# Attention values of a Macaron block: three full products per unit become four full products and two pairs over 64 rows

## The chip, the core and the metric

The kernel runs on one core of one Trainium2 chip. The metric is the device time of one execution in microseconds (us); the median of three runs is given. Inside a core the engines are TensorE (PE; its weight loads are listed apart as PEld), VectorE (DVE), ScalarE (ACT), GpSimd (POOL) and SyncE (SP), whose queue issues the DMAs. Durations of single instructions come from one profiled execution.

## The reference

Four sequences of 256 tokens, 512 features, all float32, go through half a feed-forward layer, an attention layer and half a feed-forward layer, each behind a layer norm without weights:

```python
x = x + 0.5 * ffn(layernorm(x), ...)     # base matrix + 8 low-rank experts, the top 2 chosen per token
x = x + attn(layernorm(x), wq, wk, wv, wo)
x = x + 0.5 * ffn(layernorm(x), ...)
```

The attention is what matters here. It has 32 query heads of 128 features and 8 key heads, so that 4 query heads share the keys and values of one key head. Queries and keys are rotated (rope). Token `i` sees token `j` only if `j <= i` and `j > i - 128`:

```python
scores = einsum("bqhgd,bshd->bhgqs", qg, k) * 128 ** -0.5
allowed = (j <= i) & (j > i - 128)
attn = softmax(where(allowed, scores, -inf))
out = einsum("bhgqs,bshd->bqhgd", attn, v).reshape(B, S, 4096) @ wo
```

## The kernel before, in words

The tokens are worked on in two halves `h` of two sequences each. In each half the attention goes over the 8 key heads `g`; a `group` is one `(h, g)` with its 4 query heads, and a `unit` is one `(h, g, b)`: one group and one sequence `b` of the half. There are 32 units. Products with large weights (queries, keys, values of the projection, output projection, feed-forward) are made by Strassen's scheme in Winograd's form: seven products of half size, with the sums made on POOL and DVE.

For one unit, `scores` makes the products of queries and keys in 8 blocks of 32 queries by 4 heads (128 rows). The first 4 blocks (queries 0 to 127) see the keys from 0 up to their own block; the other 4 (queries 128 to 255) see a window of 128 keys that ends in their own. `picked` and `copy_predicated` shift the windows so that a key keeps its place in its row: in a block of the second half, a column holds either the weight of an old key (0 to 127) or that of the new key 128 higher, never both. `exponentials` (ACT) writes them to `probs`, `normalize` (POOL) scales, and `turn_blocks` turns squares of 32 by 32 (DVE) and stores them to a scratch tensor `kept` in DRAM. `fetch` loads them back to `turned`, which has 128 keys on partitions, then 4 heads, 8 blocks and 32 queries; four DMAs on SP's queue, one for each 32 partitions.

`values` then multiplies by the values. `vS` holds for each sequence the values `v0` of tokens 0 to 127 and, after `difference`, the differences `v1 - v0`. Queries 0 to 127 need one product of 512 columns, `turned` blocks 0 to 3 with `v0`, in the bank `oa`. Queries 128 to 255 take two, in the bank `ob`: all of blocks 4 to 7 with `v0`, and `part` with `v1 - v0`. `part` is what `split` keeps of blocks 4 to 7: the entries that belong to new keys. `split` runs on POOL for `b == 0` (L807) and on DVE for `b == 1` (L812). Two ACT copies (L832) bring the banks to `oT`, from which `outputs` makes the sums (POOL, L126) and the seven products of the output projection (L852).

The order on PE and DVE within the units is written out by hand: in a unit with `b == 0` the letters of `order` interleave queries of the next group, the waiting output products (`late`) and the next scores; in a unit with `b == 1` the keys or the values of the projection for the next groups come in between. POOL and ACT follow the order of the code as well. Around `values` a unit runs

```python
        if not parts:
            part()
        ...
        oT = values(h, g, b, *parts)
        if b == 0 and n + 1 < len(groups):
            first, *begun = keys(*groups[n + 1]) if n % 2 == 1 else project_values(*groups[n])
            first()
```

`turn` (transposes, store and `fetch`) comes some 9 us of PE work ahead of `values` in a unit with `b == 1`. Between the two halves of the tokens `sum_tokens` makes the token sums of the second half: `t1` and `t3` on POOL, `t2` and `t4` on DVE.

Of the kernel before, what the change touches and what calls it, by code (L numbers as in the profile page):

```python
# [12 lines left out]
F32 = mybir.dt.float32  # L13
AF = mybir.ActivationFunctionType
ALU = mybir.AluOpType
AX = mybir.AxisListType

P = 128
# [20 lines left out]
def macaron_kernel(  # L39
# [154 lines left out]

    def by_heads(dst, make):
        make(dst, 0)
        other = sb.tile(list(dst.shape), F32, tag="by_heads", bufs=1, name=f"{dst.name}_hi")
        for j in range(1, G):
            make(other, j * BLK)
            nc.gpsimd.tensor_copy(dst[ts(j, BLK), :], other[ts(j, BLK), :])  # L200
# [35 lines left out]
    for c in range(1, NB):  # L236
        nc.gpsimd.memset(turned[ts(c, BLK), :, :c, :], 0.0)


    old = const.tile([P, NB, BLK], F32, name="old")  # L240
    nc.gpsimd.memset(old, 1.0)
    nc.gpsimd.affine_select(
        out=old, in_=old, compare_op=ALU.is_gt,
        fill=0.0, base=0, pattern=[[-BLK, NB], [-1, BLK]], channel_multiplier=1,
    )
    new = const.tile([P, NB, BLK], F32, name="new")
    nc.gpsimd.tensor_scalar(new, old, -1.0, 1.0, ALU.mult, ALU.add)

    rank = const.tile([P, E], F32, name="rank")
    for e in range(E):  # L250
# [18 lines left out]
    def scale(t, tag):  # L269
        if (tag, t) not in moments:  # L270
            measure(t, tag)
        mv, std = moments[tag, t]
        std = std or deviation(t, tag, mv)
        rstd = sb.tile([P, 1], F32, tag="rstd", bufs=4, name=f"rs_{tag}_{t}")
        nc.vector.reciprocal(rstd, std)
        xc = sb.tile([P, D], F32, tag="xc", bufs=3, name=f"xc_{tag}_{t}")
        if tag == "f1":
            shift = sb.tile([P, 1], F32, tag="shift", bufs=4, name=f"sh_{tag}_{t}")
            nc.vector.scalar_tensor_tensor(shift, mv[:, 0:1], -1.0, rstd, ALU.mult, ALU.mult)
            cols = slice(D // 2 if t < 2 else 0, D)  # L280
            if t < 2:
                lo = slice(0, D // 2)
                nc.vector.tensor_scalar(xc[:, lo], xt[t][:, lo], mv[:, 0:1], rstd, ALU.subtract, ALU.mult)
            nc.scalar.activation(xc[:, cols], xt[t][:, cols], AF.Identity, bias=shift, scale=rstd)
        else:
            nc.vector.tensor_scalar(xc, xt[t], mv[:, 0:1], rstd, ALU.subtract, ALU.mult)
        if far(t, tag):
            nc.vector.transpose(xc, xc)
            away = dram.tile([KC, P, P], F32, tag="away", name=f"away_{tag}_{t}")
            nc.sync.dma_start(  # L290
                out=away.rearrange("c p x -> p c x"), in_=xc.rearrange("p (c x) -> p c x", c=KC)
            )
            xc = away
        moments[tag, t] = xc

    def far(t, tag):
        return tag == ("a" if t >= TPH else "f2")
# [56 lines left out]
    def ffn(tiles, tag, then):  # L354
# [22 lines left out]
        def narrow(i):  # L377
            t = tiles[i]
            if i == 0:
                state["hl"] = sb.tile([P, TPH, E * R + E], F32, tag="hl", name=f"hl_{tag}_{t0}")[:, :n, :]  # L380
            pa = score_bank(f"pa_{tag}_{t}")
            for c in range(KC):
                nc.tensor.matmul(  # L383
                    pa[:, : E * R + E], x_of(i, c), ar_sb[:, c, :],
                    start=(c == 0), stop=(c == KC - 1),
                )
            nc.scalar.copy(state["hl"][:, i, :], pa[:, : E * R + E])
# [84 lines left out]
        def gated():  # L472
            hl = state["hl"]
            pt = ps.tile([P, n, P], F32, tag="s", bufs=4, name=f"ph_{tag}_{t0}")
            for i in range(n):
                nc.tensor.transpose(pt[:, i, :], hl[:, i, : E * R], ident)
            state["ht"] = sb.tile([P, TPH, P], F32, tag="ht", bufs=1, name=f"ht_{tag}_{t0}")
            nc.scalar.copy(state["ht"][:, :n, :], pt)

        def leave(i):  # L480
            bank, t = po.pop(i), tiles[i]
# [71 lines left out]
    def add(dst, bank, other):  # L553
        nc.vector.tensor_tensor(dst, bank, other, ALU.add)
# [111 lines left out]
    def project_values(h, g):  # L666
# [36 lines left out]
        def others():  # L703
            product(2, c11)
            product(4, c21)
            add(v21, c21, u2)
            product(3, c12)
            nc.scalar.copy(v11, c11)
            add(v12, c12, u2)
            difference(h, g)  # L710

        return first, both, second, others

# [71 lines left out]
    def turn_blocks(pr, name, c):  # L785

        if c == 0:
            kept[name] = dram.tile([P, NB, 2 * NB * BLK], F32, tag="kept", name=f"kept_{name}")
        if True:
            w = pr[:, c : c + 2].rearrange("p c n k -> p (c n k)")  # L790
            nc.vector.transpose(w, w)  # L791
            nc.sync.dma_start(
                out=kept[name][:, c : c + 2, :], in_=pr[:, c : c + 2].rearrange("p c n k -> p c (n k)")
            )

    def fetch(name):
        heads = kept.pop(name).rearrange("(j k) c x -> k j c x", j=G)
        for c in range(NB):
            nc.sync.dma_start(
                out=turned[ts(c, BLK), :, c:, :].rearrange("p j n q -> p j (n q)"),  # L800
                in_=heads[:, :, c, c * BLK :],
            )

    def split(h, g, b):
        part = sb.tile([P, G, NB, BLK], F32, tag="part", bufs=1, name=f"part_{h}_{g}_{b}")
        if b == 0 or (h, g) == groups[-1]:
            nc.gpsimd.affine_select(  # L807
                out=part, in_=turned[:, :, NB:, :], compare_op=ALU.is_ge, fill=0.0, base=0,
                pattern=[[0, G], [BLK, NB], [1, BLK]], channel_multiplier=-1,
            )  # L810
        else:
            nc.vector.tensor_tensor(  # L812
                part, turned[:, :, NB:, :], new.unsqueeze(1).to_broadcast([P, G, NB, BLK]), ALU.mult
            )
        return [turned[:, :, :NB, :]], [turned[:, :, NB:, :], part]

    def difference(h, g, tiles=slice(None)):

        pairs = vS[h, g].rearrange("p (b i) f -> p b i f", i=2)[:, tiles]
        nc.vector.tensor_tensor(pairs[:, :, 1], pairs[:, :, 1], pairs[:, :, 0], ALU.subtract)  # L820

    def values(h, g, b, p0, p1):
        oT = sb.tile([HD, G, S], F32, tag="oT", bufs=4, name=f"oT_{h}_{g}_{b}")
        v = vS[h, g - g % 2]
        cols = ts(g % 2, HD)
        for i, parts in enumerate((p0, p1)):
            po = (score_bank, mm_bank)[i](f"o{'ab'[i]}_{h}_{g}_{b}")
            for n, part in enumerate(parts):
                nc.tensor.matmul(  # L829
                    po, v[:, 2 * b + n, cols], part, start=(n == 0), stop=(n == len(parts) - 1)  # L830
                )
            nc.scalar.copy(oT[:, :, ts(i, P)], po.rearrange("p (j q) -> p j q", j=G))  # L832
        return oT

    def outputs(h, g, b, oT):
# [162 lines left out]
    def run(queue, n):  # L998
        for _ in range(min(n, len(queue))):
            queue.popleft()()  # L1000
# [24 lines left out]
    for u, (h, g, b) in enumerate(units):  # L1025
# [11 lines left out]
        def turn_half(c):  # L1037
            once(f"t{c}{ahead[-1]}", lambda: turn_blocks(ahead[0], ahead[-1], c))
# [9 lines left out]
        fill(left, 0)  # L1048
        if left == 1:
            nc.scalar.activation(root, eps, AF.Sqrt)  # L1050
        parts = []

        def look_ahead(at=u + 1):
            nonlocal ahead
# [4 lines left out]
            add_sums(h - 1, BPH - 1, nc.gpsimd, slice(-2, None))  # L1059
            sum_weights("v", *groups[n])  # L1060

        def part(at=(h, g, b)):
            parts.extend(split(*at))

        if b == 0 and n < len(groups):

            order = {0: "1n6kTvD2U75tS4r3n", 4: "1Eyn6TaW2U7cyXx5dtSy4re3yVn"}[len(late)]
            steps = queries(*groups[n], nc.scalar.copy, ends)  # L1070
            steps |= {
                "y": lambda: run(late, 1), "r": invert, "n": level, "S": look_ahead,
                "E": lambda: exponentials(*ahead, which=range(NB, 2 * NB)),
                "D": lambda: difference(0, 0, slice(1)),
                "W": lambda: sum_o_weights(h, g, ("t3", "t1")), "X": lambda: sum_o_weights(h, g, ("t2",)),
                "x": between_halves if (h, g) == groups[NKV + 1] else None,
                "V": lambda: sum_o_weights(h, g, ("t4",)), "v": lambda: project_v(0, 0, 2),
                "k": lambda: sum_weights("k", *groups[2]), "a": lambda: fill(left, 1),
                "T": lambda: turn_half(0), "U": turn, "t": part, "c": None, "d": None, "e": None,
            }  # L1080

            if g == NKV - 2 and h + 1 < NHALF:
                more_tokens = sum_tokens(h + 1, *(nc.gpsimd, nc.vector) * 2)
                steps |= {"c": more_tokens[3], "d": more_tokens[1], "e": more_tokens[2]}
            for step in order:
                if steps[step]:
# [2 lines left out]
        elif b == 1 and n + 1 < len(groups):  # L1089
# [24 lines left out]
            elif n % 2 == 0 and n + 2 < len(groups):  # L1114
                load_v(*groups[n + 2])
            run(late, len(late) - 1)
            for t in shifted:
                norm_attn(t, scaled=True)
        else:
# [15 lines left out]
            load_q(*groups[n + 1])  # L1135
        if b == 0 and 1 < n < len(groups):
            load_o(*groups[n])
        if not parts:
            part()
        fill(left, 2)  # L1140
        run(late, len(late) - 1)
        early = ahead[-1] == "{}_{}_{}".format(*units[u + 1]) if left > 1 else False
# [7 lines left out]
        if u == 0:  # L1150
            project_v(0, 0, 3)
            load_v(*groups[2])
        oT = values(h, g, b, *parts)
        if u == 0:
            difference(0, 0, slice(1, 2))
        if b == 0 and n + 1 < len(groups):

# [79 lines left out]
```

## Time and profile before

| | |
|---|---|
| median of 3 runs | 740.63 us (740.61 to 741.09) |
| profiled execution | 740.92 us, of which the span from first to last instruction is 739.2 us |
| granted TensorE clock | 1.0 |
| DVE, POOL, ACT busy | 76%, 76%, 26% of the span |
| 16 DMA engines, busy share of the main queue | 35.4% |

The span is what the views divide; 1.7 us lie around it. A product in float32 appears in the trace as two records of MATMUL, each behind a weight load of its own: the product of 512 columns in `oa` occurs 32 times and has 64 records. Records overlap at their ends, so the duration of a record is longer than the distance from one start to the next; the distance is what a product costs in a busy stretch.

### The profile page before, as it was taken

Reading aid. Unit: us, or ns where it says so; the run is one execution under the profiler, and the core shown is the slowest. Engines: PE = TensorE matmul, PEld = TensorE weight load, DVE = VectorE, ACT = ScalarE, POOL = GpSimd, SP = SyncE. Lnnn points to the kernel's source line nnn. Section 1 sums busy time; section 2 is a strip of 40 time slices with the busy share of each in tenths; the row PEclk is TensorE's granted clock in tenths of the full one; section 3 lists DMA queues with packets and bytes.
Section 4 is the critical chain, followed back from the end, with each engine's and each line's share of the span. In section 5 each row is a group of like instructions: output and inputs, shape, how many; then the busy total and the mean of one; then the engine's idle time right before and its main releaser. Section 6 shows DMA issues by size and latency. Waiting matters only on the chain.

```text
span 739.2 us, 11048 instructions
## 1 busy us (share of the span) xinstructions
PE 728.7 (99%) x3606; PEld 603.3 (82%) x3606; DVE 562.5 (76%) x1297; ACT 195.1 (26%) x724; POOL 562.1 (76%) x613
## 2 busy tenths in 40 slices
PE   8999999999999999998999999999999999999998
PEld 6878888888888888886888888888888888888766
DVE  5797895878786878778677867586877867795877
ACT  5520223332222212130222233222123031222331
POOL 6878878777968686859878699868686878976753
PEclk9999999999999999999999999999999999999999
DMA  9301251424245433625142424242332415433201
GB/s 315 141 1 37 89 177 44 155 65 152 92 155 137 149 98 107 186 69 187 53 167 70 137 83 152 81 166 80 118 129 68 150 53 177 116 124 84 71 29 58
DMA packets 78249, 83.58 MB, mean 113 GB/s; under 512 B 21232, under 2 KB 50928, under 8 KB 78192
## 3 DMA queue, kind: packets, MB, share of 16 engines
q1 hardware_dynamic: 78192, 82.87, 35.4%
q8 instruction: 29, 0.48, 0.3%
q14 instruction: 28, 0.23, 0.1%
HBM read 61.88 MB, written 20.97 MB: 112 GB/s over the span
## 4 chain that ended last, share of the span: by engine, by line
PE 84%; POOL 6%; DVE 5%; issue 3%; DMA 1%; SPq 0%; ACT 0%; DVEq 0%; POOLq 0%
PE q L575 24%; PE y L852 22%; PE ob L829 7%; PE v L684 6%; PE k L632 6%; PE sb L753 4%; PE sa L739 3%; PE oa L829 3%; PE p_f L419 3%; PE po_f L419 2%; PE po_f L482 1%; PE y L894 1%; POOL x L393 1%; PE pa_f L383 1%; PE pv L720 1%
## 5 line engine op out<-in xcount | busy, mean ns | idle before, releaser
L531 POOL TENSOR_TENSOR qT<-ra_q,rb_q 128x512 f32<-128x512 f32 x64 | 81.8, 1279 | 74.8 <-DVE rb_q L525 74.8
L525 DVE TENSOR_TENSOR rb_q<-q,sin_sb 64x512 f32<-64x512 f32 x128 | 88.1, 688 | 1.7
L772 ACT ACTIVATE probs<-probs,mx 128x32 f32<-128x32 f32 (+3 forms) x128 | 44.7, 351 | 144.8 <-DVE mx L742 144.8
L779 POOL TENSOR_TENSOR probs<-probs,sm 128x512 f32<-128x512 f32 x64 | 65.7, 1046 | 6.1 <-DVE sm L1031 6.1
L869 DVE TENSOR_TENSOR x<-y,x 128x256 f32<-128x256 f32 (+1 forms) x62 | 34.2, 551 | 41.5 <-PE y L852 41.3
L852 PE MATMUL y<-wot,oT 128*128 128x256 f32 x248 | 63.7, 379 | 0.4 <-DVE rb_q L525 0.4
L852 PE MATMUL y<-wo,oT 128*128 128x256 f32 x248 | 63.7, 379 | 0.0
L832 ACT COPY oT<-oa 128x512 f32<-128x512 f32 x32 | 18.7, 585 | 169.1 <-PE oa L829 169.1
L852 PE MATMUL y<-wo,oTs 128*128 128x256 f32 x244 | 62.6, 379 | 0.0
L575 PE MATMUL q<-xs,wq 128*128 128x256 f32 x256 | 60.6, 379 | 0.2 <-DVE rb_k L525 0.2
L575 PE MATMUL q<-xs,wqs 128*128 128x256 f32 x256 | 60.6, 380 | 0.0
L575 PE MATMUL q<-xa,wq 128*128 128x256 f32 x256 | 60.5, 379 | 0.0
L575 PEld LDWEIGHTS q<-xa,wq 128*128 128x128 f32 x256 | 48.5, 190 | 12.5 <-issue 4.1
L575 PEld LDWEIGHTS q<-xs,wqs 128*128 128x128 f32 x256 | 48.5, 190 | 7.3 <-PE y L852 0.4
L575 PEld LDWEIGHTS q<-xs,wq 128*128 128x128 f32 x256 | 48.5, 190 | 7.0 <-issue 0.5
L791 DVE STREAM_TRANSPOSE probs<-probs 128x512 f32<-128x512 f32 x64 | 43.7, 700 | 10.8 <-POOL probs L779 10.4
L852 PEld LDWEIGHTS y<-wo,oTs 128*128 128x128 f32 x244 | 46.4, 190 | 6.3
L852 PEld LDWEIGHTS y<-wot,oT 128*128 128x128 f32 x248 | 45.8, 190 | 6.5 <-POOL wot L171 0.8
L852 PEld LDWEIGHTS y<-wo,oT 128*128 128x128 f32 x248 | 45.9, 190 | 5.3
L523 DVE TENSOR_TENSOR ra_q<-q,cos_sb 128x512 f32<-128x512 f32 x64 | 43.9, 686 | 6.3 <-PE q L575 2.0
L772 ACT ACTIVATE probs<-sb,mx 128x128 f32<-128x128 f32 x128 | 44.6, 357 | 0.0
L126 POOL TENSOR_TENSOR oTs<-oT 128x256 f32<-128x256 f32 x31 | 22.9, 740 | 23.5 <-ACT oT L832 23.5
(220 smaller groups left out, 1726.7 us busy)
## 6 DMA issues: line engine op xcount, KB each, us to landing
wq<-in_wq_dram SPq DMA_DIRECT2D x16, 1024.0 KB, 5.6
wo<-in_wo_dram SPq DMA_DIRECT2D x16, 1024.0 KB, 5.2
kept<-probs SPq DMA_DIRECT2D x64, 256.0 KB, 2.2
wk<-in_wk_dram SPq DMA_DIRECT2D x8, 512.0 KB, 4.3
wv<-in_wv_dram SPq DMA_DIRECT2D x8, 512.0 KB, 4.1
turned<-kept SPq DMA_DIRECT2D x32, 128.0 KB, 2.6
turned<-kept SPq DMA_DIRECT2D x32, 112.0 KB, 2.9
turned<-kept SPq DMA_DIRECT2D x32, 96.0 KB, 2.6
```

The costliest lines, as they stand in the source:

```text
L419: nc.tensor.matmul(bank[:, ts(i, D // 2)], lhs[j][m - 1][:, c, :], weights["bs"][m - 1][:, c, :], start=(m in (1, 5, 2, 4) and c == 0), st ...
L523: nc.vector.tensor_tensor(twice(a), twice(src), angle(cos_sb), ALU.mult)
L525: nc.vector.tensor_tensor(twice(b[o : o + half, :]), twice(src[i : i + half, :]), angle(sin_sb[o : o + half, :]), ALU.mult,)
L531: nc.gpsimd.tensor_tensor(dst, view(a), view(b), ALU.add)
L575: nc.tensor.matmul(bank[:, ts(j, S)], w[:, c, ts(j, HD)], x[:, c], start=(new and j == 0 and c == 0), stop=(c == 1), skip_group_check=True,)
L632: nc.tensor.matmul(dst, w[n - 1][:, c, :], x[n - 1][:, c], start=(start and c == 0), stop=(c == 1), skip_group_check=True,)
L684: nc.tensor.matmul(bank[:, i, :], x[n - 1][:, c, i, :], w[n - 1][:, c, :], start=(start and i == 0 and c == 0), stop=(c == 1), skip_group_ ...
L772: nc.scalar.activation(dst, src, AF.Exp, bias=mx[:, n : n + 1], scale=scale, accum_out=sm[:, n : n + 1])
L779: nc.gpsimd.tensor_tensor(w, w, sm.unsqueeze(1).unsqueeze(3).to_broadcast([P, 2, 2 * NB, BLK]), ALU.mult)
L791: nc.vector.transpose(w, w)
L829: nc.tensor.matmul(po, v[:, 2 * b + n, cols], part, start=(n == 0), stop=(n == len(parts) - 1))
L852: nc.tensor.matmul(py[:, ts(i, D // 2)], lhs[n - 1][:, c, :], weights["os", h, g][n - 1][:, c, :], start=(i == 0 and c == 0), stop=(c == 1 ...
```

## The change

`values` now makes eight smaller products in two banks. Queries go by blocks of 32 (each 128 columns, with 4 heads):

- blocks 2 and 3: one full product each of 128 columns with `v0`;
- blocks 4 and 5: one full product of 256 columns with `v0`; blocks 6 and 7: one full product of 256 columns with a mixture `w` that has `v1` in rows 0 to 63 and `v0` in rows 64 to 127;
- blocks 0 and 1 see keys 0 to 63 alone: two products of 128 columns over 64 rows, one in rows 0 to 63 of the array, the other in rows 64 to 127. For the latter the keys 0 to 63 of block 1 are loaded a second time, to `aside` in partitions 64 to 127, and `vD` holds `v0` of tokens 0 to 63 there;
- `part` in rows 0 to 63 corrects blocks 4 and 5 for their new keys, in rows 64 to 127 blocks 6 and 7: two products of 256 columns over 64 rows, again one in each half of the array.

Around it: `fetch` issues four more DMAs for `part` and two for `aside`; `split` masks `part` in place, half as wide; `mixture` makes `w` and `vD` with three ACT copies per pair of groups; there are four ACT copies of 256 columns to `oT` instead of two of 512. `difference` moves from `others` to the end of the unit's work before the mask. `t2` of `sum_tokens` moves from DVE to POOL. Several tiles take over the buffers of others to make room (`xc` those of `ra`, `rb` and `u2`; `hl` those of `v`; `ht` those of `z16`).

```diff
+    low, high = slice(0, P // 2), slice(P // 2, P)
+    new = const.tile([P, NB // 2, BLK], F32, name="new")
...
+    part = const.tile([P, G, NB // 2, BLK], F32, name="part")
+    aside = const.tile([P, G, BLK], F32, name="aside")
...
-        xc = sb.tile([P, D], F32, tag="xc", bufs=3, name=f"xc_{tag}_{t}")
+        home, bufs = (("xc", "u2"), 1) if far(t, tag) else (("ra", "rb"), 2)
+        xc = sb.tile([P, D], F32, tag=home[t % 2], bufs=bufs, name=f"xc_{tag}_{t}")
...
             nc.scalar.copy(v11, c11)
             add(v12, c12, u2)
-            difference(h, g)
+            mixture(h, g)
...
     def fetch(name):
...
+        for c in range(NB):
+            n = NB + c - c % 2
+            nc.sync.dma_start(
+                out=part[ts(c, BLK)].rearrange("p j n q -> p j (n q)"),
+                in_=heads[:, :, c, n * BLK : (n + 2) * BLK],
+            )
+        for c in range(2):
+            nc.sync.dma_start(out=aside[high][ts(c, BLK)], in_=heads[:, :, c, BLK : 2 * BLK])
 
     def split(h, g, b):
-        part = sb.tile([P, G, NB, BLK], F32, tag="part", bufs=1, name=f"part_{h}_{g}_{b}")
-        if b == 0 or (h, g) == groups[-1]:
-            nc.gpsimd.affine_select(
-                out=part, in_=turned[:, :, NB:, :], compare_op=ALU.is_ge, fill=0.0, base=0,
-                pattern=[[0, G], [BLK, NB], [1, BLK]], channel_multiplier=-1,
-            )
-        else:
-            nc.vector.tensor_tensor(
-                part, turned[:, :, NB:, :], new.unsqueeze(1).to_broadcast([P, G, NB, BLK]), ALU.mult
-            )
-        return [turned[:, :, :NB, :]], [turned[:, :, NB:, :], part]
+        engine = nc.gpsimd if b == 0 or (h, g) == groups[-1] else nc.vector
+        engine.tensor_tensor(part, part, new.unsqueeze(1).to_broadcast([P, G, NB // 2, BLK]), ALU.mult)
+
+    def mixture(h, g, tiles=slice(None)):
...
+        pairs = vS[h, g].rearrange("p (b i) f -> p b i f", i=2)[:, tiles]
+        for i, rows in ((1, low), (0, high)):
+            nc.scalar.copy(vW[h, g][rows, tiles], pairs[rows, :, i])
+        nc.scalar.copy(vD[h, g][high, tiles], pairs[low, :, 0])
 
-    def values(h, g, b, p0, p1):
+    def values(h, g, b):
         oT = sb.tile([HD, G, S], F32, tag="oT", bufs=4, name=f"oT_{h}_{g}_{b}")
-        v = vS[h, g - g % 2]
-        cols = ts(g % 2, HD)
-        for i, parts in enumerate((p0, p1)):
-            po = (score_bank, mm_bank)[i](f"o{'ab'[i]}_{h}_{g}_{b}")
-            for n, part in enumerate(parts):
-                nc.tensor.matmul(
-                    po, v[:, 2 * b + n, cols], part, start=(n == 0), stop=(n == len(parts) - 1)
-                )
-            nc.scalar.copy(oT[:, :, ts(i, P)], po.rearrange("p (j q) -> p j q", j=G))
+        at, cols = (h, g - g % 2), ts(g % 2, HD)
+        v0, dv = (vS[at][:, 2 * b + i, cols] for i in range(2))
+        w, v0_low = vW[at][:, b, cols], vD[at][high, b, cols]
+        pa, pb = (make(f"o{c}_{h}_{g}_{b}") for c, make in (("a", score_bank), ("b", mm_bank)))
+        n = G * BLK
+
+        def add(dst, v, p, start=False, stop=False):
+            nc.tensor.matmul(dst, v, p, start=start, stop=stop, skip_group_check=True)
+
+        add(pb[:, n : 2 * n], v0, turned[:, :, 3, :], start=True, stop=True)
+        add(pa[:, n : 2 * n], v0, turned[:, :, 2, :], start=True, stop=True)
+        add(pb[:, 2 * n :], w, turned[:, :, 6:8, :])
+        add(pa[:, 2 * n :], v0, turned[:, :, 4:6, :])
+        add(pa[:, :n], v0[low], turned[low, :, 0, :], stop=True)
+        add(pb[:, :n], v0_low, aside[high], stop=True)
+        add(pa[:, 2 * n :], dv[low], part[low], stop=True)
+        add(pb[:, 2 * n :], dv[high], part[high], stop=True)
+        blocks_of = oT.rearrange("p j (n q) -> p n j q", q=BLK)
+        for i, po in enumerate((pa, pb)):
+            nc.scalar.copy(blocks_of[:, i:NB:2], po[:, : 2 * n].rearrange("p (n j q) -> p n j q", n=2, j=G))
+        for i, po in enumerate((pa, pb)):
+            nc.scalar.copy(
+                oT[:, :, P + i * S // 4 :][:, :, : S // 4], po[:, 2 * n :].rearrange("p (j q) -> p j q", j=G)
+            )
         return oT
...
-            order = {0: "1n6kTvD2U75tS4r3n", 4: "1Eyn6TaW2U7cyXx5dtSy4re3yVn"}[len(late)]
+            order = {0: "1n6kTvD2U75tS4r3n", 4: "1Eyn6TaW2U7cyXx5dteSy4r3yVn"}[len(late)]
...
-                more_tokens = sum_tokens(h + 1, *(nc.gpsimd, nc.vector) * 2)
+                more_tokens = sum_tokens(h + 1, *(nc.gpsimd,) * 3, nc.vector)
...
             run(late, len(late) - 1)
+            if n % 2 == 0:
+                difference(*groups[n])
```

Order of the eight products, for later reference: 1 and 2 are the full ones of 128 columns, 3 and 4 the full ones of 256, 5 and 6 the pair of 128 over 64 rows, 7 and 8 the pair of 256 over 64 rows. Everything else on PE keeps its order.

## The prediction

> **What bounds the kernel now.** I read the page's busy times first, then the chain of work that ended last, then the timeline of TensorE around one unit, then the waits and the transfers of that unit.
>
> ```profile
> PE 728.7 (99%) x3606; PEld 603.3 (82%) x3606; DVE 562.5 (76%) x1297; ACT 195.1 (26%) x724; POOL 562.1 (76%) x613
> PE 84%; POOL 6%; DVE 5%; issue 3%; DMA 1%; SPq 0%; ACT 0%; DVEq 0%; POOLq 0%
> ```
>
> The last chain is TensorE for 84% of the span, and in the waits of PE no item of the steady stretch is over 1 us in sum. So a microsecond less on PE is a microsecond less at the end, as long as no other engine comes up behind it; DVE and POOL have a quarter of their time left.
>
> ```profile
> 427.53 1.03 PE L852 MATMUL y<-wo,oTs 128*128 128x256 f32 x4
> 428.39 1.05 PE L739 MATMUL sa<-kT,qT 128*128 128x32 f32 x8
> 429.29 1.25 PE L753 MATMUL sb<-kT,qT 128*128 128x160 f32 x8
> 430.38 1.03 PE L852 MATMUL y<-wot,oT 128*128 128x256 f32 x4
> 431.24 1.03 PE L852 MATMUL y<-wo,oTs 128*128 128x256 f32 x4
> 432.10 1.02 PE L829 MATMUL oa<-turned,v 128*128 128x512 f32 x2
> 432.96 1.02 PE L829 MATMUL ob<-turned,v 128*128 128x512 f32 x2
> 433.82 1.02 PE L829 MATMUL ob<-part,v 128*128 128x512 f32 x2
> 434.68 1.67 PE L575 MATMUL q<-xa,wq 128*128 128x256 f32 x7
> ```
>
> Start to start is the price. A product of 512 columns (two records) costs 0.86 us, so the three of a unit cost 2.58 us (432.10 to 434.68). Two products of 256 (x4) cost 0.86, so one costs 0.432. The scores `sa` have 32 to 128 columns, and still their 8 records take 0.90, 0.112 each: under 128 columns the price stops falling, each record having a weight load of its own.
>
> ```profile
> 141.76 4.46 PE v L684 x40
> ```
>
> This piece of the chain in order of time gives a record of 128 columns: 4.46 / 40 = 0.1115, a product 0.223.
>
> **The products.** The full ones cost 2 x 0.223 + 2 x 0.432 = 1.31 us. The two pairs, run one product after the other, cost again 1.31, for a row of the array takes no part in the price (only columns do in the rows above, as an estimate for 64 rows too). Together 2.62, 0.04 more than before: +1.3 us over 32 units. All gain is thus overlap of the halves of the array, and no row of this trace has a product over 64 rows. Bounds: none, +1.3 us; total, where a pair takes the time of one, 1.31 + 0.655 = 1.965, that is -0.615 x 32 = -19.7 us. I take a middle for a reason that the rows show: each product is two records, and on PE records start in program order. The order is low, low, high, high; the second low record may run with the first high one, but the first low has no partner and the last high none either. Three times in place of four: 0.75 x 1.31 = 0.983, a unit 2.293, -0.287 x 32 = **-9.2 us**.
>
> [...]
>
> **Changes between the whole array and halves.** There are two per unit, 64 in all. The lower bound is the row above where the shape of the operands changes: `sa` to `sb`, `sb` to `y`, `y` to `oa` follow at their pace, within 0.02 us. The upper bound is a pipeline that runs empty: a last record of 512 columns lasts 0.592 (1.02 - 0.43), 0.16 longer than its pace, and a restart after a wait costs 0.11 more, as here, where four records take 0.97 to the next start and not 0.86:
>
> ```profile
> 343.38 1.13 PE L632 MATMUL k<-xa,wk 128*128 128x256 f32 x4 [0.82 <-DVE v_k L554]
> 344.35 0.81 PE L632 MATMUL k<-xs,wk 128*128 128x256 f32 x3
> ```
>
> That is 0.27 x 64 = 17.3 us against 0.02 x 64 = 1.3. I take 0.05 each, near the rows without a wait: **+3.2**.
>
> [...]
>
> **Loads.** `fetch` grows from 4 to 10 DMAs, all on SP's queue, behind the wait for `kept`.
>
> ```profile
> 425.83 1.74 SPq L799 DMA_DIRECT2D turned<-kept  x4
> 430.75 0.69 DVE L812 TENSOR_TENSOR part<-turned,new 128x512 f32<-128x512 f32 x1 [0.53 <-DMA turned<-kept]
> ```
>
> One issue takes 1.74 / 4 = 0.44 us. The mask starts when the last block of `turned` has landed (430.7). Four more issues bring `part` to about 432.4, two more `aside` to 433.3. Mask in place, half as wide: between 0.42 (the 256 wide reduction L762) and 0.69, so ready at about 433.0. PE wants `aside` for product 6 at 432.10 + 1.31 + 0.22 = 433.63 and `part` for product 7 a little later: 0.3 and 0.8 us to spare. In the units with `b == 0` the mask runs some 5 us ahead of its product. So 16 units are exposed; their price is between nothing and about 1 us each (the landings spread from 2.2 to 5.1 us). I take 0.05: **+0.8**. Behind the mask on DVE wait the row maxima of the next scores (L742), up to 1.7 us later than now; ACT's exponentials wait for them, and the 5 us of the next unit cover that. Without that cover it is again up to 1 us in a unit. Weight loads behind the six new issues come 2.6 us later; the page's medians of 5 us to landing and their use a unit later hide it.
>
> **Copies and sums.** ACT makes four copies of 256 columns, 0.372 each by L691, in place of two of 0.585: +0.32 x 32 = 10 us, and 24 copies of `mixture` at up to 0.585, 14 us, on an engine that is busy for 26%: nothing on PE. `oT` is complete some 0.5 us later; the first output product comes 1.73 us after `values`, which covers it. After the last unit nothing covers it: L894 follows at once and must wait for the copy after product 8, 0.16 + 0.37 + the signal: **+0.6**, once. The mask saves DVE some 0.3 x 15 and costs POOL nothing (0.73 for the affine select, 0.74 for a sum of 256 columns in L126): no PE time. `difference` waits for `mixture` on ACT, but far ahead of its use: nothing. `t2` leaves DVE, where a wait of 0.43 (PE y L852 on rb_q at 339.74) stands behind it, for POOL, whose sums come 1.27 later: between -0.6 and +1.3, I take 0. The shared buffers: `xc` has fewer buffers for the transposed tiles and each waits for its store (2.4 us to landing), with several us between them: between 0 and 2, I take 0.
>
> **Sum.** -9.2 + 3.2 + 0.8 + 0.6 = -4.6. From the profiled 740.92 that is 736.3; the median of the runs is 0.3 below that execution, so **736.0 us**.
>
> **Rivals.**
>
> Whole overlap: a pair costs one product. For it: two halves of the array have no row in common, and their products go to different banks. Against: two records per product in program order. -19.7 + 3.2 + 1.4 = -15.1, 725.5 us.
>
> The change of shape empties the array. Place: product 5 after 4, and the first product of the next step after 8. Price 0.27 x 64 = 17.3: -9.2 + 17.3 + 1.4 = +9.5, 750.1 us. It decides from (9.2 - 1.4) / 64 = 0.12 us per change on. For it: a restart in this trace does cost that much. Against: no change of operand shape does.
>
> The halves take turns: the change doesn't do what it says. +1.3 + 3.2 + 1.4 = +5.9, 746.5 us. For it: weight loads of 0.19 us that follow each other at 0.11; a pair of 128 columns has four of them, 0.45 us, which is all that the pair costs unpaired. Against: pairs of 256 need 0.45 for loads and 0.86 unpaired, so there is room.
>
> Loads decide: half a us in each of the 16 units, -5.4 + 8 = +2.6, 743.2 us; with 0.34 each it comes out even.
>
> **Chances.** Forecast 0.36, whole overlap 0.18, emptied array 0.26, turns 0.12, loads 0.08. Of the emptied array 0.03 and of the loads 0.05 fall near the point of no change, which is 0.2% (1.5 us), about what a measurement of this kernel can tell. Faster 0.54, same 0.08, slower 0.38. The forecast's own range, from the bounds of its small terms, is 730 to 739. The whole range must reach into the whole overlap on one side and over the emptied array on the other: 723 to 752, with less than 0.1 outside at each end.
>
> **What would show it.** Between the start of product 1 and the next step's first record: 2.3 us (forecast), 2.0 (whole), 2.6 (turns), over 2.6 (emptied). Records of `oa` and `ob` over 64 rows that start together show overlap. A gap of over 0.1 us ahead of product 5 and after 8 shows the emptied array. Waits of PE for `aside`, `part` or DMA in units with `b == 1` show the loads. I am wrong in kind if PE's steady stretch keeps its 39 us per group, or if POOL or DVE take over the chain between units.

## The result, and the profile after

The changed kernel takes 746.06 us (median of 4 runs, 744.36 to 747.27) against 740.63 before: a ratio of 1.007, 95% interval 1.005 to 1.009. It is slower, and the forecast of 736.0 had the wrong sign. The profiled execution took 745.94, with a span of 744.2 (739.2 before).

The page's busy times and its row of the granted TensorE clock (one digit for each fortieth of the span):

```profile
PE 727.9 (98%) x3926; PEld 622.5 (84%) x3926; DVE 559.7 (75%) x1296; ACT 210.2 (28%) x815; POOL 558.2 (75%) x615
PEclk9999999999999999999999999999999999999899
```

PE is busy for 0.8 us less and the span is 5.0 longer: on balance, PE stands still for 5.8 us more. No other engine took over. One digit of the clock is an 8, in the slice from 688 to 707. These two readings lead to the two parts of the story, a gain in every unit and a loss in one place near the end.

**The gain.** TensorE's timeline around `values` (L848) of unit 17, the unit that the prediction showed:

```profile
430.53 0.38 PE L848 MATMUL ob<-turned,v 128*128 128x128 f32 x2
430.75 0.39 PE L848 MATMUL oa<-turned,v 128*128 128x128 f32 x2
430.98 0.60 PE L848 MATMUL ob<-turned,vw 128*128 128x256 f32 x2
431.41 0.90 PE L848 MATMUL oa<-turned,v 128*128 128x256 f32 x3
431.94 0.37 PE L848 MATMUL ob<-aside,vd 64*128 64x128 f32 x1
432.15 0.27 PE L848 MATMUL oa<-turned,v 64*128 64x128 f32 x1
432.16 0.27 PE L848 MATMUL ob<-aside,vd 64*128 64x128 f32 x1
432.26 0.38 PE L848 MATMUL oa<-part,v 64*128 64x256 f32 x1
432.27 0.38 PE L848 MATMUL ob<-part,v 64*128 64x256 f32 x1
432.48 0.38 PE L848 MATMUL oa<-part,v 64*128 64x256 f32 x1
432.49 0.38 PE L848 MATMUL ob<-part,v 64*128 64x256 f32 x1
432.79 1.13 PE L582 MATMUL q<-xa,wq 128*128 128x256 f32 x4
```

From the first value product to the next step it is 2.26 us, where it was 2.58. Every record over 64 rows has a partner in the other half of the array, 0.01 us behind it: both records of product 5 with both of product 6 (the first of product 5 is counted in the x3 of the line above), both of 7 with both of 8. In the whole trace 114 of the 128 pairs of such records start 0.01 us apart. The pairs overlap wholly.

The price stands in the weight loads of the same stretch (the bracket is the idle time ahead of a load):

```profile
431.20 0.41 PEld L848 LDWEIGHTS oa<-turned,v 128*128 128x128 f32 x2
431.94 0.18 PEld L848 LDWEIGHTS oa<-turned,v 64*128 64x128 f32 x1 [0.33 <-issue]
432.79 0.94 PEld L582 LDWEIGHTS q<-xa,wq 128*128 128x128 f32 x5 [0.33 <-issue]
```

Elsewhere in this unit a load starts 0.1 to 0.2 us ahead of its record (431.20 for the product at 431.41). At the two changes of shape the loads stand idle for 0.33 and then start with their record. In the whole trace the idle time is 0.33 at 62 of 66 changes, and at none of them does a load start ahead of its record. The first record behind a change comes about 0.1 late, and the second another 0.1, as its load is late too (431.94 to 432.15 for 128 columns, 0.21, where 0.11 is the pace). So a change costs 0.2 us here, a unit 0.4, and 0.1 of that falls behind the 2.26, in the next step. In all a unit comes out 0.21 us shorter. The start of `values` against before moves by just that in each unit of the steady stretch (unit 6 to 12: from +0.43 to -0.84), and at unit 30 the changed kernel is 3.04 us ahead.

**The loss.** At unit 31 it is 3.40 us behind. TensorE's timeline of unit 30 and the start of unit 31, first before:

```profile
686.45 1.10 PE L829 MATMUL oa<-turned,v 128*128 128x512 f32 x2 [0.50 <-issue]
687.38 1.02 PE L829 MATMUL ob<-turned,v 128*128 128x512 f32 x2
688.79 1.12 PE L829 MATMUL ob<-part,v 128*128 128x512 f32 x2 [0.38 <-POOL part L807]
689.75 1.03 PE L419 MATMUL p_f<-wb_sb,xn_f 128*128 128x256 f32 x4
...
704.50 1.02 PE L829 MATMUL oa<-turned,v 128*128 128x512 f32 x2
```

and after:

```profile
683.41 0.46 PE L848 MATMUL oa<-turned,v 128*128 128x128 f32 x2 [0.79 <-DMA turned<-kept]
686.62 2.05 PE L426 MATMUL p_f<-wb_sb,xn_f 128*128 128x256 f32 x4 [2.75 <-DVE mx L749]
688.46 0.64 PE L848 MATMUL ob<-turned,v 128*128 128x128 f32 x2
...
691.45 1.53 PE L426 MATMUL p_f<-wbs_wk,xs_f 128*128 128x256 f32 x4
692.91 0.48 PE L848 MATMUL oa<-part,v 64*128 64x256 f32 x1
...
694.67 1.13 PE L426 MATMUL p_f<-wbs_wk,xs_f 128*128 128x256 f32 x4 [0.84 <-ACT oT L862]
...
707.90 0.49 PE L848 MATMUL oa<-turned,v 128*128 128x128 f32 x2
```

and two stretches by windows, the granted clock behind the busy times of the five engines:

```profile
675.00:683.00 8.00, 7.62 (x50) 6.94 (x48) 7.01 (x15) 1.13 (x3) 7.84 (x10) 1.00 0.73 183
685.50:692.20 6.70, 5.58 (x14) 4.12 (x15) 3.56 (x20) 0.00 (x0) 2.79 (x3) 0.50 0.00 0
```

The order here is not the hand-written one. The order by hand ends when three units are left (`in_order.close()`), and from there the scheduler places the eight products one by one, as it sees fit. It put a product of the feed-forward, `p_f`, behind the first value product. `p_f` needs a bank that DVE still reads for row maxima (`mx`, L749), so PE stands for 2.75 us with seven value products queued behind. During that wait, at 685.5, the clock falls to 0.50, and it stays there until 692.3. The four records of `p_f` take 1.84 us to the next start, against 0.97 for four of them at 694.67. The same products up to 691.45 take some 2.6 at full pace (read from e9 below) and 4.83 here: 2.2 lost. The second `p_f`, at 691.45, still starts at half clock: 1.46 to the next start, against 0.96 for the same records in the same place in e9, 0.5 lost. With 0.84 for `oT` this is 6.3 of the 6.4 us that are lost between the units. (The second `p_f` also parts product 5 from product 6; what that alone costs can't be told apart here.) Before, the scheduler had three large products to place and kept them ahead of `p_f`.

Smaller losses occur once. At 102 us an output product waits 0.91; the profile names the keys' copy on ACT (`p1c_k`, L648), which now stands behind `mixture`'s copies for unit 0, but `rb_q` on DVE (L532) ends only 0.06 us ahead of it, and e6 below decides between the two. The products of unit 31 take 3.90 us to the next step where they took 2.58, and 0.46 of that is the wait of L926 for `oT`.

### The profile page after: what moved, and what is told of

Its sections match the earlier page's. It is cut to its first block, busy times and chain, and to the rows that moved or that the text cites. A ratio compares the mean times of both kernels' runs of the same rounds, so it can differ in the third digit from the quotient of the medians.

```text
span 744.2 us, 12138 instructions
## 1 busy us (share of the span) xinstructions
PE 727.9 (98%) x3926; PEld 622.5 (84%) x3926; DVE 559.7 (75%) x1296; ACT 210.2 (28%) x815; POOL 558.2 (75%) x615
## 4 chain that ended last, share of the span: by engine, by line
PE 82%; DVE 5%; POOL 5%; issue 4%; SPq 1%; ACT 1%; DMA 1%; DVEq 0%; POOLq 0%; ACTq 0%
PE q L582 24%; PE y L884 23%; PE v L691 6%; PE k L639 6%; PE oa L848 6%; PE sb L760 4%; PE sa L746 3%; PE ob L848 3%; PE p_f L426 2%; PE po_f L426 2%; PE y L926 1%; PE pv L727 1%; PE pa_f L390 1%; SPq L311 1%; PE po_f L489 1%
## 5 line engine op out<-in xcount | busy, mean ns | idle before, releaser
L532 DVE TENSOR_TENSOR rb_q<-q,sin_sb 64x512 f32<-64x512 f32 x128 | 88.1, 688 | 1.7
L860 ACT COPY oT<-oa 128x256 f32<-128x256 f32 x32 | 11.9, 373 | 208.5 <-PE ob L848 154.8
L582 PE MATMUL q<-xa,wq 128*128 128x256 f32 x256 | 62.1, 386 | 0.1
L848 PE MATMUL oa<-turned,v 128*128 128x128 f32 (+2 forms) x192 | 45.6, 331 | 0.8 <-DMA turned<-kept 0.8
```

The source lines that it names most:

```text
L532: nc.vector.tensor_tensor(twice(b[o : o + half, :]), twice(src[i : i + half, :]), angle(sin_sb[o : o + half, :]), ALU.mult,)
L582: nc.tensor.matmul(bank[:, ts(j, S)], w[:, c, ts(j, HD)], x[:, c], start=(new and j == 0 and c == 0), stop=(c == 1), skip_group_check=True,)
L848: nc.tensor.matmul(dst, v, p, start=start, stop=stop, skip_group_check=True)
```

## The experiments

Each kernel was timed beside the kernel before, which took 740.88, 740.92 and 740.86 us (median) in the three jobs. e1 and e9 start from the changed kernel, e10 from e6, all others from e1; they are told in the order of what they settle.

**e1: TensorE held by hand to the end.** DVE is released at three units as in the changed kernel, PE is not:

```diff
         if left == 3:
             in_order.close()
+            in_order.enter_context(tc.manual_schedule(engines={mybir.EngineType.PE}))
...
+    in_order.close()
     f2 = [ffn(tiles(last[0], b, 1), "f2", store) for b in range(BPH)]
```

> The changed kernel, with PE alone kept in the order of the code through the last three units (in_order closes three units before the end and lets the scheduler order PE and DVE; here PE stays by hand). On PE nothing moves but the products of units 30 and 31. Theory A: up to unit 29 the change gains 3 us, and the order that the scheduler gives PE in units 30 and 31 loses them and 5 more (a product of the feed-forward part between the first two value products waits 2.75 us for VectorE, and TensorE then runs at half clock for some 5 us). Then this kernel takes 738.5 us (737 to 740.5), faster than before. Theory B: the loss at the end lies in the later loads, the mask and the four copies of these units, whatever the order: 744 to 745.5 us.

Measured 738.91 us (737.5 to 740.8, 11 runs), ratio 0.9974 (0.9966 to 0.9983). 7.15 us come back with nothing changed but the order of a few products on PE in the last units. The theory holds: the change as such is a gain, and the scheduler's order in the last units made it a loss. (The two medians are of different jobs, in which the kernel before differs by 0.25.) In unit 30 the first value product still waits, 1.37 in place of 0.79 and 2.75, and the clock stays up. The releaser that the profile names, DVE's `r_f`, ended just then, and the last block of `turned` landed 0.14 us ahead; these products read only the latter:

```profile
684.62 0.46 PE L848 MATMUL ob<-turned,v 128*128 128x128 f32 x2 [1.37 <-DVE r_f L340]
...
687.62 1.13 PE L426 MATMUL p_f<-wb_sb,xn_f 128*128 128x256 f32 x4
```

**e9: one product moved.** In the last three units `values` alone is held on PE (`with tc.manual_schedule(...): oT = values(h, g, b)`), the rest is the scheduler's. Against the changed kernel this moves the first `p_f` of unit 30 from behind the first to behind the fifth value product, and swaps neighbours.

> The changed kernel with the eight products of a unit kept together in the last three units up to product 5; the scheduler keeps all the rest. In unit 30 this moves one product of two records, p_f of wb_sb and xn_f, from behind the first value product to behind the fifth, and swaps neighbours among the value products; else TensorE's order is that of the changed kernel. Theory: p_f cannot start before DVE has taken the row maxima (686.6 in the changed kernel), and all that costs there is that six value products, ready at 684.5, stand behind it. Behind five of them it waits under 1.5 in place of 2.75, the granted clock stays up, and most of the 7.2 us between the changed kernel (746.06) and e1_pe_held (738.91) comes back: 739 to 740.5. Rival: the place of p_f matters little as it still waits ahead of products 6 to 8; the loss comes from the rest of the scheduler's order in unit 30, above all the second p_f (of wbs_wk) among the pairs: 743 to 746.

Measured 741.31 us (739.4 to 742.61, 11 runs), ratio 1.0005 (0.9996 to 1.0013). The place of that one product is worth 4.75 of the 7.15 us. There it finds its bank free and waits for nothing:

```profile
685.71 1.13 PE L426 MATMUL p_f<-wb_sb,xn_f 128*128 128x256 f32 x4
...
703.99 0.46 PE L848 MATMUL ob<-turned,v 128*128 128x128 f32 x2 [1.30 <-DVE mv_f L266]
```

The other 2.4 go to the rest of the scheduler's order: the third `p_f` still waits 0.85 for `oT`, and unit 31 starts behind a wait of 1.30 that e1 does not have (the last block of `turned` lands 0.19 us ahead of its end). The theory's range, 739 to 740.5, was too low and the rival's, 743 to 746, too high; both causes exist, the first is twice the second.

**e2: no halves.** Products 5 to 8 over all 128 rows; the number and the width of the products stay. It leaves out the split of `part` by halves and serves for its time alone:

```diff
-        add(pa[:, :n], v0[low], turned[low, :, 0, :], stop=True)
-        add(pb[:, :n], v0_low, aside[high], stop=True)
-        add(pa[:, 2 * n :], dv[low], part[low], stop=True)
-        add(pb[:, 2 * n :], dv[high], part[high], stop=True)
+        add(pa[:, :n], v0, turned[:, :, 0, :], stop=True)
+        add(pb[:, :n], v0, turned[:, :, 1, :], stop=True)
+        add(pa[:, 2 * n :], dv, part, stop=True)
+        add(pb[:, 2 * n :], dv, part, stop=True)
```

> As the run with PE held, but products 5 to 8 go over all 128 rows (5 and 6 with blocks 0 and 1 of turned, 7 and 8 with all rows of part, so that the second half's queries come out wrong): same eight products, same columns, same loads, copies and masks, no halves and no change of shape. If the gain of the steady stretch is the overlap of the halves, the values of a unit take 2.62 us in place of 2.37 with what follows: +0.25 x 32 = +8, 746.5 us (745 to 748), slower than before. If the halves were worth nothing and the gain lay in masks or order: within 1 us of the run with PE held.

Measured 745.01 us (744.74 to 745.8, 5 runs), ratio 1.0056 (1.0044 to 1.0068). From the first value product to the next step a unit takes 2.62 us:

```profile
434.32 0.38 PE L848 MATMUL ob<-turned,v 128*128 128x128 f32 x2
...
436.94 0.38 PE L582 MATMUL q<-xa,wq 128*128 128x256 f32 x1
```

The units drift by +0.05 us each against before, where e1's drift by -0.21. So the halves, overlap less changes, are worth 0.26 us in a unit and 6.1 in the medians; the prediction's +0.04 for eight products without overlap is confirmed.

**e4: four changes of shape.** Product 4 goes between the pairs: 5, 6, 4, 7, 8. Same products, two more changes in a unit.

> As the run with PE held, but product 4 (whole array) stands between the two pairs: four changes between the whole array and halves in a unit instead of two. If each change costs what the trace shows (0.10 us on the way in, 0.09 + 0.11 on the way out), a unit loses 0.3 us more: +9.6 us against the run with PE held (7 to 11), about 748. If that loss belongs to the pairs and not to the change of shape (weight loads behind the pair of 128 columns): within 3 us.

Measured 752.62 us (750.95 to 754.91, 4 runs), ratio 1.016 (1.0144 to 1.0176). In the steady stretch a unit is 0.40 us longer than in e1: 0.20 for a change, which is the reading of the weight loads above, by another way. Over 32 units that is 12.8 of the 13.7 between the medians, more than the 7 to 11 that I expected. TensorE's timeline:

```profile
437.38 0.60 PE L848 MATMUL ob<-turned,vw 128*128 128x256 f32 x2
437.91 0.37 PE L848 MATMUL oa<-turned,v 64*128 64x128 f32 x1
438.12 0.27 PE L848 MATMUL oa<-turned,v 64*128 64x128 f32 x1
438.33 0.70 PE L848 MATMUL oa<-turned,v 128*128 128x256 f32 x2
438.96 0.48 PE L848 MATMUL oa<-part,v 64*128 64x256 f32 x1
```

Product 4 alone takes 0.63 to the next start (438.33 to 438.96), against 0.43 for 256 columns amid others: 0.20 more.

**e3: low, low, high, high.** The order 5, 7, 6, 8: the two products of one half of the array follow each other. If records started in program order, no pair could overlap by more than one record.

> As the run with PE held, but the four products over 64 rows in the order 5, 7, 6, 8: low, low, high, high. If records start in program order across the halves, as the prediction assumed, only the last low record overlaps the first high one: the four take 1.08 us instead of 0.75, +0.33 x 32 = +10.5 us against the run with PE held, about 749. If each half has an order of its own and a high product passes a waiting low one, the four take the same 0.65 to 0.75 us: within 1 us of the run with PE held.

The overlap stays whole. Products 5 and 6 still start together, though 7 was issued between them:

```profile
431.52 0.27 PE L848 MATMUL oa<-turned,v 64*128 64x128 f32 x1
431.54 0.27 PE L848 MATMUL ob<-aside,vd 64*128 64x128 f32 x1
431.63 0.38 PE L848 MATMUL oa<-part,v 64*128 64x256 f32 x1
431.65 0.38 PE L848 MATMUL ob<-part,v 64*128 64x256 f32 x1
```

Each half keeps an order of its own in these rows, and the units move by the same -0.21 as in e1. It was otherwise where data were late: in unit 12, where product 7 waits for the mask, product 6 stands behind it in the queue and waits too, though its own data landed 5 us before:

```profile
335.09 0.48 PE L848 MATMUL oa<-part,v 64*128 64x256 f32 x1 [0.59 <-POOL part L820]
335.20 0.46 PE L848 MATMUL ob<-aside,vd 64*128 64x128 f32 x2
```

The median is 740.56 us (738.35 to 743.51, 12 runs), ratio 1.0 (0.9989 to 1.0011), 1.65 over e1 and so over the 1 us that I had allowed; its profiled span is only 0.3 over e1's, and where the median loses the rest is not settled.

**e11: the loads' margin.** The four transfers of `part` are issued twice in each unit.

> e1_pe_held (738.91) with the four transfers of part issued twice in every unit, the same data to the same place: 1.76 us more of SP's queue ahead of the mask and of aside. Asks how far the loads were from deciding. In e1_pe_held aside lands 0.4 to 1.7 us ahead of product 6 in the units with b = 1, and the mask ends 0.1 to 1.5 ahead of product 7. Theory (the spare is what the landings show, and no more): the excess of 1.76 over the smaller spare, summed over 14 such units, is 12, and about 1.5 each in the last two units, 15 in all: 751 to 754. Rival: the landings, not the issues, are in line one after the other, so that twice the issues bring less than 1.76, or PE takes the waits up elsewhere: 740 to 745.

Measured 780.05 us (774.19 to 781.54, 6 runs), ratio 1.0518 (1.0494 to 1.0543): +41 where 12 to 15 was expected. From the waits of PE:

```profile
PE ob L849 <- DMA aside<-kept: 23.3, 15, 2.3
```

23.3 us of waits in 15 units. Behind four of them the granted clock is 0.50 for 3.4 us each, and near the end once for 6.8 (20.5 in all; about half of that is lost, as four records take 1.84 at 0.50 in unit 30 of the changed kernel and 0.97 at 1.00). With some 0.3 for the tail ahead of each wait and the restart behind it, an estimate from e8 below, this is 38 of the 41. The issues were underestimated too: in unit 3 it is 6.7 us from the first issue of `turned` to the landing of `aside` in e1, 9.0 here, 2.4 for four issues and not 1.76. The rival is out, and the theory was far too low. In e1 `aside` has a margin of 0.4 to 1.7 in the units with `b == 1` up to unit 27; in unit 30 it has none, and product 6 starts some 0.6 us late. Behind the margin lies a price of over 1 us in each unit with `b == 1`.

**e8: a wait in the steady stretch.** Six copies of half of `oT` onto itself on ACT behind unit 17:

```diff
         oT = values(h, g, b)
+        if u == 17:
+            for _ in range(6):
+                nc.scalar.copy(oT[:, :, :P], oT[:, :, :P])
```

> e1_pe_held with six further copies of half of oT onto itself on ACT after unit 17's values, the result unchanged: the first output product there, 2 us behind the values, has to wait for them. Asks what one wait of TensorE costs. Six copies of 512 columns are 3.5 us, so the wait is 2.5 to 3. Theory: a wait of this length is followed by records at half pace, as behind the 2.75 us of the changed kernel at 686.6 (0.43 between records of 256 columns in place of 0.216): another 3 to 4.5 us are lost, the median goes from 738.9 to 744.5 to 746.5, and the granted clock falls in that slice. Rival: the wait costs itself and 0.11 for the restart, 741.5 to 742, and the slow records of the changed kernel's unit 30 come from something else there, the transposed tiles' other products or late operands.

Measured 742.14 us (740.68 to 744.5, 12 runs), ratio 1.0016 (1.0006 to 1.0025), 3.2 over e1. Against e1 the units fall back by 3.0 at this place. TensorE's timeline and the window behind the wait:

```profile
439.72 1.99 PE L582 MATMUL q<-xa,wq 128*128 128x256 f32 x8 [2.39 <-ACT p1c_q L597]
```

```profile
440.00:444.00 4.00, 4.00 (x20) 3.51 (x20) 2.29 (x5) 1.06 (x7) 2.78 (x4) 1.00 0.00 0
```

My theory, that a wait of this length brings half pace behind it, falls. This one cost its 2.39, some 0.3 for the tail ahead of it and the restart behind it (the eight records ahead take 1.89 to their end, the eight behind it 1.83 to the next start, against 1.73 at their pace), and a second short stop at 445.3 (0.4); the clock stayed at 1.00. That some waits bring half pace and others do not is taken up in the last section.

**e5, e6 and e7: the small waits.** e6 puts `mixture(0, 0, slice(1, 2))` and `difference` of unit 0 behind `first()`, so that ACT makes `p1c_k` first. e7 puts, between the halves of the tokens, the mask ahead of POOL's `t1` and `t2` back on DVE. e5 has both.

> e1_pe_held with unit 0's second mixture behind the keys' copy, alone. Theory: y L884 no longer waits for p1c_k (0.91 at 102.7), the units after it start 0.9 sooner, the median is 738.0. Rival: the gain is given back at a later wait (unit 30): 738.7 to 739.0.

> e1_pe_held with the mask ahead of t1 on POOL and t2 on DVE between the halves, alone. Theory: the waits of 0.60 (part) and 0.99 (wot) between 336 and 341 shrink to 0.3 together or less, the units after them start 1.2 sooner, median 737.7. Rival for the prediction's zero for t2: t2 on DVE delays rb_q or the scores there by as much (the kernel before shows such waits of 0.59, 0.99 and 0.77), sum even, 738.5 to 739.3.

> TensorE held by hand to the end (as in e1_pe_held, 738.91), and three one-time waits taken up: unit 0's second mixture goes behind the keys' copy p1c_k, which costs TensorE 0.91 in e1_pe_held; between the halves the mask goes ahead of POOL's sum t1 (TensorE waits 0.60 for the mask there) and t2 goes back to DVE (TensorE waits 0.99 for wot, on POOL behind t2). Theory: each of these waits is met by nothing else and comes off the end nearly whole: -0.9 and -0.6 to -1.6, a median of 736.5 to 737.5. Rival: TensorE only waits for the next late thing, as at unit 30 (a lead of 2.83 becomes 1.83 at a wait of 1.37 for turned): what is gained early is given back there, and the median stays at 738.4 to 739.

e6: 738.72 us (737.73 to 741.74, 10 runs), ratio 0.9974 (0.9964 to 0.9984), no different from e1. The rival's time holds, its reason does not: nothing is given back later, for the wait itself stays. `p1c_k` is there over 1 us sooner, and the product waits as long, for DVE:

```profile
102.75 1.10 PE L884 MATMUL y<-wot,oT 128*128 128x256 f32 x4 [0.91 <-DVE rb_q L532]
```

e7: 739.71 us (738.08 to 742.84, 12 runs), ratio 0.9989 (0.9978 to 1.0). e5: 740.04 (739.03 to 743.83, 12 runs), ratio 0.9991 (0.9981 to 1.0001). Both are about 1 us worse than e1, and worse than any case written down for them. DVE, with `t2`, delivers `xs` and `rb_q` later, and PE waits 0.97 (0.96 in e5) and 1.63 for them; between units 12 and 13 e5 loses 0.7 us against the kernel before, where e1 wins 0.4. So `t2` was better off on POOL. The two kernels have the same two waits in this place, and the windows behind them (e5 first, then e7) differ in one column:

```profile
341.00:344.00 3.00, 2.73 (x13) 2.07 (x12) 2.66 (x6) 0.00 (x0) 2.84 (x4) 1.00 0.00 0
```

```profile
341.00:344.00 3.00, 3.00 (x9) 2.38 (x8) 1.50 (x4) 0.00 (x0) 2.92 (x3) 0.50 0.00 0
```

The clock was granted in full in one execution and by half in the other, and the lead at unit 13 differs by 1.2 us for it.

**e10: POOL's order between the halves.** The mask ahead of `t1`, the sum `wot` ahead of the last `qT`, `t2` on POOL.

> e6_mixture_later (738.72) with, between the halves alone, the mask ahead of POOL's t1 and the sum wot ahead of the last qT; t2 stays on POOL. Theory: the waits of 0.60 (part) and 0.99 (wot) are POOL's order alone and both go: 737.2 to 737.6, the lead of the units from 13 on grows by 1.2 to 1.5. Rival: the output product then waits for rb_q, as in e5_three_small and e7_half_boundary, or the next scores wait for qT, which comes 1.3 later: 738 to 740.

Measured 738.83 us (737.5 to 741.01, 12 runs), ratio 0.9975 (0.9966 to 0.9985). Both waits for POOL are gone from its profile, and 1.3 us are won between units 12 and 13; at unit 14 0.5 is given back, in place of the 0.2 that a unit gains (queries wait 0.51 for `rb_q` there), so that it ends where e6 is. The rival's time holds, and DVE's `rb_q` is what decides, though at another product than the one that I named. e1, e6 and e10 beat the kernel before by 0.25% to 0.26%, and are alike.

## Why the prediction was wrong

**The sum of the steady stretch was right, its two large terms were not.** Products: I took half the overlap, -9.2, because records would start in program order. The pairs overlap wholly (2.26 us less 0.3 of the changes inside is the 1.965 of the whole overlap), -0.615 x 32 = -19.7; e3 refutes the reason. Changes of shape: I took 0.05 each, +3.2, near the rows where the operands change without a wait. They cost 0.20 each, +12.8 (weight loads idle for 0.33, and e4). Together -6.9 against -6.0: the 2.26 us of the timeline match the 2.3 that I gave as the forecast's mark, and would have passed as a proof of it. That is luck: neither step was right, and two errors cancel. The rivals each held half of the truth, whole overlap and a dear change of shape (0.20 against the 0.12 from which the emptied array was to decide; that the array empties, no run shows), and I had no case with both.

**The small terms.** Loads: I put +0.8; in the changed kernel they and the mask cost some 0.1 in each of units 5, 15 and 25. In the other units with `b == 1`, up to unit 27, the spares are 0.5 to 1.9 us where 0.3 and 0.8 were worked out, and the doubt was well placed (e11). The copies of `oT` at the end: +0.6, measured 0.5 to 0.7. In unit 0 the sum has nothing where 0.84 is lost: `mixture` stands ahead of `p1c_k` on ACT there, but e6 shows that DVE's `rb_q` alone holds the product as long. Why it holds it here, and not in the kernel before, stays open. `t2`: between units 12 and 13 the changed kernel's lead grows by 0.42, 0.2 more than a unit gives; the 0 stood between its bounds.

**The step that failed is one that the sum didn't have.** It multiplied a unit's gain by 32, and the description of the change said that all else on PE keeps its order. It does for units 0 to 29. In the last ones the scheduler decides, and eight small products give it more places to put others between than three large ones; why it chose this place, no run shows. That was +7.15 us (changed kernel against e1, by medians), of which one product's place is 4.75. Without it the change gives 738.91 - 740.88 = -2.0 us. From the -6.7 of 32 units to that -2.0 there are waits of 0.1 to 1.4 us that the earlier PE runs into, the largest at unit 30 (the landing of `turned`, and of `aside` behind it), at unit 1 and at the end. The forecast had given the tail copy alone for them; its time for this case, 736.0, would have been 2.9 too low.

The measured 746.06 is near the rival "halves take turns" (746.5), and has nothing to do with it.

## What to carry to other kernels

Where a hand-written order ends and a scheduler takes over, splitting an instruction into many can change the order of all that stands there; list the order of the changed kernel there before the gain of a unit is multiplied by all units. Two products over different halves of the array's rows cost the time of one here (starts 0.01 to 0.02 us apart), in both orders that were tried, as long as neither waits for its data; but each change between whole array and halves cost 0.2 us: group the halves, and count the changes. A forecast's total can be met by two errors that cancel, so let each term have a mark of its own in the trace (here the starts of the pairs, and the idle time of the weight loads).

## What the runs showed of the hardware

- In the trace of the changed kernel 114 of the 128 pairs of records over rows 0 to 63 and 64 to 127 start 0.01 us apart. In e3 they start 0.02 us apart, although another product of the first half was issued between them. Where product 7 waited 0.59 us for its data, product 6 of the other half, issued behind it and with its own data there, started 0.11 us behind it (e3, unit 12).
- In unit 17 of the changed kernel a weight load starts 0.1 to 0.2 us ahead of its record. At 62 of the 66 changes between whole array and halves in this trace the loads stand idle for 0.33 us, and at all 66 the first load behind the change starts with its record. Two more changes in a unit cost 0.40 us of PE time, 0.20 for each (e4).
- Behind some waits of PE the granted clock was halved, and behind others it was not: in unit 30 of the changed kernel it fell during a wait of 2.75 us (0.50 from 685.5 to 692.3), in e8 it stayed at 1.00 behind 2.39 us, and behind the same pair of waits, 0.97 (0.96 in e5) and 1.63 with four records between them, it was 0.50 in e7 and 1.00 in e5 (341 to 344). So in these runs it was not the length of the waits alone; what decided, they don't show.
